# Expert layer of the second sequence and channel mix of the first, issued in pieces among the second attention's groups, with GELU and sigmoid written through tanh

## The chip, the cores and the metric

The kernel runs on one core of a Trainium2 chip. The metric is device time in microseconds (us): the median of the timed executions. A separate execution was recorded by the hardware profiler, and every duration and start time in this document comes from such a record.

The engines are named as in the profile: PE is TensorE (PEld its weight loads), DVE VectorE, ACT ScalarE, POOL GpSimd, and SP the engine that issues most of the DMAs. Each engine runs its own queue in order.

## The reference

Two sequences of 1024 tokens with 128 channels, all in f32, pass through four residual layers. Each layer reads a layer norm of x and adds its result to x.

```python
x = x + attn0(norm(x))   # 16 heads of 64, rotary embedding, full softmax over 1024 keys
x = x + ffn0(norm(x))    # 8 experts, each token goes to one:
                         #   y = gelu_tanh(t @ w1[e] + b1[e]) @ w2[e] + b2[e], times its route probability
x = x + attn1(norm(x))   # 16 heads of 8; keys of later 32-token windows get score 0 and still count
x = x + ffn1(norm(x))    # channel mix: r = sigmoid(xr @ W_r); k = relu(xk @ W_k)**2; r * (k @ W_v)
                         #   xr, xk blend each token with the one before it
```

GELU is the tanh approximation, 0.5 h (1 + tanh(sqrt(2/pi) (h + 0.044715 h^3))). The sigmoid equals 0.5 (1 + tanh(z/2)).

## The kernel before

The program is written with a tile framework. Python code issues instructions with tile names; a scheduler then fixes the order of each engine's queue from a cost model. Among the instructions that the model finds ready it takes the one issued first in the program. Tiles of one tag share a fixed number of buffers (`bufs`), and an instruction that needs a buffer still in use waits for the last reader. Semaphores are added by the framework.

**First attention** (`project`, `scores`, `flip`, `weighted`, `projected`). It walks 128 steps: 2 sequences x 8 head pairs x 8 query blocks. Beside the steps of the second sequence, the dictionary `beside` hangs the pieces of the expert layer of the first sequence, at hand-written step numbers.

**Expert layer** (`switch(b, ...)`). It returns three lists. `first_part` is `norm` (layer norm "f"), two `turn` pieces (transposes on PE), `route` (softmax over 8 experts and the argmax), `sort` (each token's slot in a list of 15 blocks of 128 rows), and eight `send` pieces: indirect DMAs from POOL that scatter 128 rows each into a DRAM tile `rows` (L298). `by_unit` has 8 units of two blocks (the last has one). In a unit `load` fetches the sorted rows (L310) and reads the block's expert number into a register of SP, with which it fetches 578 KB of weights per block (L314). `across` transposes the rows, `up` multiplies by w1 and adds the bias (L331), and after its last block runs GELU on ACT (L334). `down` multiplies by w2, adds the bias (L345) and stores to the DRAM tile `done` (L347). The third list gathers from `done` (`back`, L351) and adds to x (L356).

For the second sequence the same three lists run in a section of their own, between the two attentions, with two buffers of rows and four of weights.

**Second attention.** `prepare(b)` makes the layer norm "u", the q and k channels (`channels`, L649), splits each into three bf16 parts (`split`, L658 and L660), writes the parts to DRAM (`kept`, L666), and computes values and the sums for keys out of reach (`values`, `suffix`, `unreached`). `spread(n)` reads the parts back from DRAM in another layout, with 18 DMAs per group (L713). A group n is four heads of one sequence, so there are 8 groups. `maxima(n)` computes scores on PE and the row maxima on DVE (L738), and `rows_of` sends these by DMA into the `side` tiles (L758). `sums(n)` computes transposed scores `sT`, the exponentials on ACT (L782), and the weighted sums `o` on PE. `close(b)` divides and applies the output projection.

All of these pieces are placed by due times in a list `plan`, in units of a group: `maxima(n)` from n - 1.2 to n - 0.2, `sums(n)` from n to n + 1, and pieces of `prepare(1)` from 0.05 on. The list is sorted and issued. In this section every PE instruction is issued through `keep_in_program_order`, so the PE queue has exactly the order of the plan.

**Channel mix**, the last section: for each sequence a layer norm "z", transposes, two blends with the preceding token on DVE (L915, L917), three matrix products, relu and sigmoid on ACT (L924, L932), the square on POOL (L926), and the store.

Of the kernel before, what the change touches and what calls it, by code (L numbers as in the profile page):

```python
# [32 lines left out]
EPS = 1e-5  # L33
BIG = 1e30
# [3 lines left out]
def block_kernel(ctx: ExitStack, tc: tile.TileContext, t: dict, out: bass.AP):  # L38
# [27 lines left out]

    def mm(o, lhsT, rhs, start=True, stop=True):
        nc.tensor.matmul(o, lhsT, rhs, start=start, stop=stop)  # L68
# [92 lines left out]
    def transposed(xn, dst, name, affine=None):  # L161

        for g in range(2):
            pt = psum_t(f"pt_{name}_{g}")
            for c in range(4):
                nc.tensor.transpose(pt[:, c, :], xn[:, 4 * g + c, :], ident)
            o = dst[:, g * HALF : (g + 1) * HALF]
            i = pt.rearrange("p c k -> p (c k)")
            if affine is not None:
                nc.vector.tensor_scalar(o, i, affine[:, 0:1], affine[:, 1:2], ALU.mult, ALU.add)  # L170
            elif g == 0:
                nc.vector.tensor_copy(o, i)
            else:
                nc.scalar.copy(o, i)
# [16 lines left out]
    def switch(b, fp, deep):  # L191
# [6 lines left out]
        def r3(name, dtype=F32):  # L198
            return fp.tile([P, NCH, E], dtype, tag=name, name=f"{name}_{b}", bufs=1)
# [14 lines left out]
        def turn(g):  # L214
            pt = psum_t(f"pt_f_{b}_{g}")
            for c in range(4):
                nc.tensor.transpose(pt[:, c, :], state["xn"][:, 4 * g + c, :], ident)
            nc.scalar.copy(state["xT"][:, g * HALF : (g + 1) * HALF], pt.rearrange("p c k -> p (c k)"))

        def route():  # L220
# [20 lines left out]
            eq = r3("eq")  # L241
            tt(eq, prob, over_e(pmax), ALU.is_equal)
            cand = r3("cand")
# [7 lines left out]
        def sort():  # L251
# [16 lines left out]
            over = fp.tile([P, E, NCH], F32, tag="over", name=f"over_{b}", bufs=1)  # L268
# [3 lines left out]
            part = fp.tile([P, E, E], F32, tag="part", name=f"part_{b}", bufs=1)  # L272
# [5 lines left out]
            at = r3("at")  # L278
            nc.vector.scalar_tensor_tensor(at, over_c(begin), float(P), rank, ALU.mult, ALU.add)
            mine = r3("mine")  # L280
# [23 lines left out]
        ins, weights, xTs, hids = {}, {}, {}, {}  # L304

        def load(u):
            n = len(units[u])
            ins[u] = fp.tile([P, 2, D], F32, tag="rows", name=f"in_{b}_{u}", bufs=deep)
            k0 = units[u][0] * P
            nc.sync.dma_start(ins[u][:, :n], rows[k0 : k0 + n * P, :].rearrange("(c p) d -> p c d", p=P))  # L310
            for k in units[u]:
                e = nc.sync.value_load(state["whose"][0:1, k : k + 1], min_val=0, max_val=E - 1)
                weights[k] = fp.tile([P, FFN], F32, tag="wts", name=f"wts_{b}_{k}", bufs=2 + deep)
                nc.sync.dma_start(weights[k], t["ffn"][bass.ds(e, 1), :, :].rearrange("o p n -> (o p) n"))  # L314

        def across(u):
            n = len(units[u])
            pt = psum_t(f"pt_x_{b}_{u}")
            for i in range(n):
                nc.tensor.transpose(pt[:, i, :], ins[u][:, i, :], ident)  # L320
            xTs[u] = fp.tile([P, 2, P], F32, tag="xTs", name=f"xTs_{b}_{u}")
            nc.vector.tensor_copy(xTs[u][:, :n], pt[:, :n])
            hids[u] = fp.tile([P, 2, NFC, P], F32, tag="hid", name=f"hid_{b}_{u}", bufs=deep)

        def up(u, i):
# [7 lines left out]
            if i == n - 1:  # L333
                nc.scalar.activation(hids[u][:, :n], hids[u][:, :n], AF.Gelu_apprx_tanh)  # L334

        def down(u):
            n = len(units[u])
            py = psum_t(f"py_{b}_{u}")
            yo = fp.tile([P, 2, D], F32, tag="yrows", name=f"yo_{b}_{u}")
            for i, k in enumerate(units[u]):  # L340
# [4 lines left out]
                tt(yo[:, i, :], py[:, i, :], w[:, 2 * F + NFC :], ALU.add)  # L345
# [3 lines left out]
        def back(c):  # L349
            y = fp.tile([P, D], F32, tag="y", name=f"y_{b}_{c}", bufs=2 * deep)  # L350
            nc.gpsimd.indirect_dma_start(  # L351
                out=y, out_offset=None, in_=done[:, :],
                in_offset=bass.IndirectOffsetOnAxis(ap=state["place"][:, c : c + 1], axis=0),
            )
            xc = x[:, b * NCH + c, :]
            nc.vector.scalar_tensor_tensor(xc, y, state["gate"][:, c : c + 1], xc, ALU.mult, ALU.add)  # L356
# [6 lines left out]
            + [lambda u=u: down(u)]  # L363
            for u in range(len(units))
        ]
        return first_part, by_unit, [lambda c=c: back(c) for c in range(NCH)]
# [7 lines left out]
    with (  # L374
# [135 lines left out]
        early_part, units, back = switch(0, fp0, 1)  # L510
        at = NPAIR * NCH + NCH + LAG + 1
        for i, f in enumerate(early_part):
            beside.setdefault(at + (i if i < 5 else 5 + (i - 5) // 2), []).append(f)
        at += 13
        for u, fs in enumerate(units):
            for j, f in enumerate(fs):
                beside.setdefault(at + 5 * u + (-4 if j == 0 else 4 if j == len(fs) - 1 else j - 1), []).append(f)
# [23 lines left out]
        for work in later + sum(beside.values(), []) + back:  # L541
            work()

    first.close()

    with (
        tc.tile_pool(name="ffn", bufs=2) as fp0,
        tc.tile_pool(name="ps_t2", bufs=8, space=PSUM) as ps_t,
    ):
        banks.update(t=ps_t, w=ps_t)  # L550
        early_part, units, last = switch(1, fp0, 2)
        for f in early_part:
            f()
        for u in range(len(units) + 2):
            if u < len(units):
                units[u][0]()
            if 1 <= u <= len(units):
                for f in units[u - 1][1:-1]:
                    f()
            if u >= 2:  # L560
                units[u - 2][-1]()
        for f in last:
            f()
# [14 lines left out]
    with (  # L578
        tc.tile_pool(name="at1", bufs=2) as bp,
        tc.tile_pool(name="dr1", bufs=1, space=bass.MemoryType.DRAM) as dr1,  # L580
# [14 lines left out]
        def mm(o, lhsT, rhs, start=True, stop=True):  # L595
            return tc.keep_in_program_order(nc.tensor.matmul(o, lhsT, rhs, start=start, stop=stop))  # L596

        def flip1(o, i, one):
            return tc.keep_in_program_order(nc.tensor.transpose(o, i, one))
# [23 lines left out]
        def prepare(b):  # L623

            uT = acts.tile([P, N], F32, tag="xT", name=f"xT_u_{b}")
            work = []

            def norm():
                un = normed(b, "u")
                xs = x[:, seq(b), :]  # L630
                nc.gpsimd.tensor_tensor(xs, xs, bo1[:, None, :].to_broadcast([P, NCH, D]), ALU.add)
                for g in range(2):
                    work.insert(g, lambda g=g: turn(un, g))

            def turn(un, g):
                pt = psum_b(f"pt_u_{b}_{g}")
                for c in range(4):
                    flip1(pt[:, c, :], un[:, 4 * g + c, :], ident)
                nc.scalar.copy(uT[:, g * HALF : (g + 1) * HALF], pt.rearrange("p c k -> p (c k)"))

            full = {}

            def channels(which, g):
                if g == 0:
                    full[which] = bp.tile([P, N], F32, tag="full", name=f"full_{b}_{which}")
# [8 lines left out]
            def split(which):  # L654
                ps = [bp.tile([P, N], BF16, tag=f"part{which}{i}", name=f"part_{b}_{which}_{i}", bufs=1) for i in range(3)]
# [23 lines left out]
            def suffix():  # L679
                later = bp.tile([P, NCH - 1, H1, DA], F32, tag="later", name=f"later_{b}", bufs=1)  # L680
# [14 lines left out]
            work += [norm]  # L695
            work += [lambda w=w, g=g: channels(w, g) for w in range(2) for g in range(2)]
            work += [lambda w=w: split(w) for w in range(2)]
# [17 lines left out]
        def maxima(n):  # L715
# [35 lines left out]
            def rows_of():  # L751
# [3 lines left out]
                nT = bp.tile([3 * HG, N], BF16, tag="nT", name=f"nT_{n}")  # L755
# [14 lines left out]
        def sums(n):  # L770
# [29 lines left out]
            def turned(half):  # L800
# [9 lines left out]
                far = bp.tile([P, 4, HG, DA], F32, tag="far", name=f"far_{n}_{half}")  # L810
# [27 lines left out]
        def close(b):  # L838

            cx = cxs[b]  # L840
            cn = bp.tile([P, NCH, H1, DH1], F32, tag="cn", name=f"cn_{b}", bufs=1)

            def divide():
                r = small.tile([P, NCH, H1], F32, tag="r1", name=f"r1_{b}")
# [8 lines left out]
            def turn1(g):  # L853
                pc = psum_b(f"pc_{b}_{g}")
                for c in range(4):
                    flip1(pc[:, c, :], cn[:, 4 * g + c].rearrange("p h d -> p (h d)"), ident)
                cTs[g] = bp.tile([P, 4, P], F32, tag="cT", name=f"cT_{b}_{g}")
# [10 lines left out]

        def run(work):
# [4 lines left out]

        AHEAD = 0.2
        work = prepare(0)
        run(work)
        for n in range(2):
            spread(n)
        plan = []  # L880
        for n in range(B * NG):
            plan += [(n - 1 - AHEAD + at, f) for at, f in maxima(n)]
            plan += [(n + at, f) for at, f in sums(n)]
            if n >= 2:
                plan.append((n - 2 + 0.3, lambda n=n: spread(n)))
        work = prepare(1)

        def first_of_second():
            work.pop(0)()

        plan += [(0.05 + 0.055 * i, first_of_second) for i in range(len(work) + 2)]
        plan += [(NG + 0.4 + 0.05 * i, f) for i, f in enumerate(close(0))]
        plan.sort(key=lambda e: e[0])
# [3 lines left out]


    with (
        tc.tile_pool(name="ffn1", bufs=2) as gp,  # L900
        tc.tile_pool(name="ps_s3", bufs=2, space=PSUM) as ps_s,
        tc.tile_pool(name="ps_t3", bufs=2, space=PSUM) as ps_t,
        tc.tile_pool(name="ps_m3", bufs=2, space=PSUM) as ps_m,
    ):
        banks.update(s=ps_s, t=ps_t, m=ps_m)
        rest = gp.tile([P, 2], F32, tag="rest", name="rest", bufs=1)
        nc.vector.tensor_scalar(rest, mu, -1.0, 1.0, ALU.mult, ALU.add)
        for b in range(B):
            zT = gp.tile([P, N + 1], F32, tag="zT", name=f"zT_{b}")
            nc.gpsimd.memset(zT[:, 0:1], 0.0)  # L910
            transposed(normed(b, "z"), zT[:, 1:], f"z_{b}")
            mix = []
            for w in range(2):
                prev = gp.tile([P, N], F32, tag=f"prev{w}", name=f"prev{w}_{b}")
                nc.vector.tensor_scalar_mul(prev, zT[:, :N], rest[:, w : w + 1])  # L915
# [118 lines left out]
```

## Time and profile before

| what | us |
|---|---|
| median of 3 runs (1522.61 to 1526.13) | 1526.01 |
| profiled execution, its own time | 1524.13 |
| its span, first to last instruction | 1522.3 |
| end of the last score matrix work of attention 1 (last `ptt`) | about 1007 |
| first `in<-rows` load of the second sequence's experts | 1061.7 |
| last `py` matmuls of that expert layer | 1138.8 |
| first `sT` matmul of the second attention | 1206.9 |
| last `oS` copy of the second attention | 1482.2 |

Busy shares over the span: PE 89%, DVE 61%, ACT 48%, POOL 28%. To read the profile: a row of instructions gives line, engine, operation, the tile written and the tiles read, the count, busy time and mean duration, and then how long the engine stood idle before them and what ended that idle time. PEclk is the clock that PE was granted, as a fraction of full speed; matmul durations at a clock below 1 are longer. PE's busy time is modelled, so 90% does not mean that PE works at its peak.

### The profile page before, as it was taken

How to read it: one execution, taken by the hardware profiler on the slowest of the kernel's cores; microseconds unless marked ns; L12 is line 12 of the kernel's file. 1: busy time of each engine (PE TensorE's matmuls, PEld its weight loads, DVE VectorE, ACT ScalarE, POOL GpSimd, SP SyncE). 2: the span in 40 equal slices, each digit the busy share in tenths (PEclk: the TensorE clock that was granted, in tenths of full speed). 3: DMA queues.
4: the chain of work that ended last, by engine and by line, in shares of the span. 5: the costliest groups of instructions: out<-in, count | busy, mean ns of one | idle time of the engine just before them, and what ended most of it. 6: DMA issues, size and time to landing. Idle time of an engine off the chain costs nothing.

```text
span 1522.3 us, 22391 instructions
## 1 busy us (share of the span) xinstructions
PE 1350.8 (89%) x8418; PEld 773.9 (51%) x8418; DVE 923.2 (61%) x1859; ACT 737.1 (48%) x1383; POOL 429.9 (28%) x422
## 2 busy tenths in 40 slices
PE   3999999999999999999999999980674889898975
PEld 2455565565565565565666666660562233333324
DVE  6656665666666666656555565652225886787716
ACT  0555455455545555455554555640112166666672
POOL 2443434333443333453332332232005010000001
PEclk9999999999999999999999999985676599999997
DMA  5000000000000000100111111002334222211000
GB/s 182 1 2 0 1 1 1 1 1 1 1 1 1 1 1 1 55 11 5 39 39 39 39 39 37 5 17 83 110 107 141 45 65 38 44 33 33 2 2 28
DMA packets 34037, 47.61 MB, mean 31 GB/s; under 512 B 4101, under 2 KB 22021, under 8 KB 33801
## 3 DMA queue, kind: packets, MB, share of 16 engines
q1 hardware_dynamic: 32329, 42.50, 10.0%
q0 software_dynamic: 1024, 2.10, 0.4%
q8 instruction: 67, 1.10, 0.3%
q10 hardware_dynamic: 576, 1.57, 0.3%
q14 instruction: 41, 0.34, 0.1%
HBM read 36.79 MB, written 9.18 MB: 30 GB/s over the span
## 4 chain that ended last, share of the span: by engine, by line
PE 77%; DMA 7%; DVE 7%; ACT 5%; issue 2%; POOL 1%; SPq 0%; POOLq 0%; ACTq 0%; DVEq 0%
PE ptt L467 16%; PE s L68 16%; PE ov L68 15%; PE pq L68 8%; PE o L596 4%; ACT pT L782 3%; PE s L596 3%; PE sT L596 3%; DVE nm L738 2%; PE py L68 2%; PE pv L68 2%; PE ph L68 2%; DMA wts<-in_ffn 2%; PE y L68 2%; DMA rows<-xn_f,place 1%
## 5 line engine op out<-in xcount | busy, mean ns | idle before, releaser
L443 DVE TENSOR_SCALAR_CACHE_REDUCE neg<-s 128x1024 f32<-128x1024 f32 x256 | 303.3, 1222 | 222.6 <-PE s L68 222.6
L447 ACT ACTIVATE p<-neg,nm 128x1024 f32<-128x1024 f32 x256 | 293.2, 1147 | 234.5 <-DVE neg L443 232.7
L452 POOL TENSOR_SCALAR p<-p,r 128x1024 f32<-128x1024 f32 x256 | 283.9, 1122 | 353.5 <-PE ptt L467 227.6
L467 PE MATMUL ptt<-ident,p 128*128 128x128 f32 x2048 | 269.2, 280 | 3.2 <-POOL p L452 2.0
L68 PE MATMUL s<-qkT,qkT 64*128 64x512 f32 x1024 | 259.9, 615 | 0.7 <-DVE neg L443 0.6
L467 PEld LDWEIGHTS ptt<-ident,p 128*128 128x128 f32 x2048 | 219.1, 140 | 75.6 <-issue 49.2
L68 PE MATMUL ov<-pT,v 128*64 128x256 f32 x2048 | 255.7, 386 | 0.0
L470 DVE COPY pT<-ptt 128x512 f32<-128x512 f32 x256 | 177.1, 692 | 120.0 <-PE ptt L467 112.4
L738 DVE TENSOR_REDUCE nm<-s 128x1 f32<-128x640 f32 (+7 forms) x176 | 175.3, 1025 | 59.2 <-PE s L596 57.6
L472 ACT COPY pT<-ptt 128x512 f32<-128x512 f32 x256 | 148.3, 586 | 114.8 <-PE ptt L467 114.2
L782 ACT ACTIVATE pT<-sT 128x512 f32<-128x512 f32 (+3 forms) x384 | 161.8, 493 | 84.5 <-PE sT L596 83.5
L68 PEld LDWEIGHTS ov<-pT,v 128*64 128x64 f32 x2048 | 138.5, 136 | 97.2 <-issue 31.1
L417 POOL TENSOR_TENSOR qkT<-rp,rp 128x512 f32<-128x512 f32 x64 | 81.6, 1275 | 255.5 <-DVE rp L412 251.0
L68 PEld LDWEIGHTS s<-qkT,qkT 64*128 64x128 f32 x1024 | 89.5, 186 | 84.0 <-issue 81.8
L596 PEld LDWEIGHTS <-side 107*128 107x128 bf16 (+1 forms) x768 | 66.4, 100 | 129.0 <-issue 86.8
L596 PE MATMUL sT<-side,side 107*128 107x512 bf16 (+3 forms) x384 | 99.7, 330 | 19.5 <-ACT pT L782 16.2
L596 PE MATMUL s<-side,side 104*128 104x512 bf16 (+3 forms) x384 | 99.4, 359 | 11.4 <-DMA side<-kept 5.9
L412 DVE SCALAR_TENSOR_TENSOR rp<-pq,rope 128x512 f32<-128x512 f32 x128 | 85.2, 685 | 2.3 <-PE pq L68 2.1
L811 POOL TENSOR_TENSOR far<-oor,en 128x144 f32<-128x144 f32 x16 | 7.0, 441 | 273.1 <-ACT en L809 208.6
L596 PE MATMUL o<-pT,v 128*32 128x512 f32 (+3 forms) x768 | 81.8, 499 | 0.0
L68 PE MATMUL pq<-xT_a,w_qkv 128*128 128x512 f32 x128 | 72.4, 648 | 0.0
L68 PE MATMUL pq<-xT_a,w_swap 128*128 128x512 f32 x128 | 68.9, 620 | 0.0
(173 smaller groups left out, 1015.6 us busy)
## 6 DMA issues: line engine op xcount, KB each, us to landing
wts<-in_ffn SPq DMA_DIRECT2D x30, 578.0 KB
side<-kept SPq DMA_DIRECT2D x144, 64.0 KB
kept<-part SPq DMA_DIRECT2D x12, 256.0 KB
rows<-zero SPq DMA_DIRECT2D x2, 960.0 KB
in<-rows SPq DMA_DIRECT2D x14, 128.0 KB
done<-yo SPq DMA_DIRECT2D x14, 128.0 KB
w_qkv<-in_w_qkv ACTq DMA_DIRECT2D x3, 512.0 KB
x<-in_x SPq DMA_DIRECT2D x2, 512.0 KB
```

Source lines behind the costliest of these rows:

```text
L68: nc.tensor.matmul(o, lhsT, rhs, start=start, stop=stop)
L412: nc.vector.scalar_tensor_tensor(part, pq, DH0 ** -0.5 if which == 0 else 1.0, rope[:, s, tok], ALU.mult, ALU.mult)
L417: nc.gpsimd.tensor_tensor((qT, kT)[which][:, tok], parts[0], parts[1], ALU.add)
L443: nc.vector.tensor_scalar(neg, s[:, j].rearrange("p g k -> p (g k)"), -1.0, None, ALU.mult, ALU.min, accum_out=nm)
L447: nc.scalar.activation(p, neg, AF.Exp, bias=nm, scale=-1.0, accum_out=sums[:, j : j + 1])
L452: nc.gpsimd.tensor_scalar(out[j], out[j], r[:, j : j + 1], 1.0, ALU.mult, ALU.mult)
L467: nc.tensor.transpose(pt[:, c, :], probs[j][:, c0 : c0 + P], ident)
L470: nc.vector.tensor_copy(o, pt)
L472: nc.scalar.copy(o, pt)
L596: return tc.keep_in_program_order(nc.tensor.matmul(o, lhsT, rhs, start=start, stop=stop))
L738: nc.vector.tensor_reduce(o, sv, AX.X, ALU.max, negate=True)
L782: nc.scalar.activation(pT[:, :w], s[:, :w], AF.Exp)
```

## The change

1. The section between the attentions is gone. The first sequence's `back` and its layer norm "u" (now a function `enter`) are put among the last steps of the first attention, and the expert units there are 4 steps apart instead of 5.
2. The second sequence's `first_part` is issued in turn with the second half of `prepare(0)`. Its 8 units get due times from -0.78 to 1.82 in the plan, its gathers and additions follow, then `enter(1)` and `prepare(1)` from 2.17 to 3.2.
3. GELU by one ACT instruction becomes a chain of five: Square on ACT, two POOL instructions, Tanh on ACT, one on DVE. The sigmoid of the channel mix becomes Tanh with scale 0.5, its factor and sum folded into DVE instructions that were there.
4. The store of a unit's result is a piece of its own, a fifth of a unit after `down` (one step later in the first attention). The gathers are split from the additions.
5. `mix(b)` is the channel mix in 11 pieces; those of sequence 0 are due from 4.8 on, 0.12 apart, and those of sequence 1 run at the end. The first factor of a blend moves from DVE to POOL.
6. Expert matmuls, transposes and channel mix in this section also go through `keep_in_program_order` and take their PSUM tiles from the three `ps1_t` banks that `sT` uses. Several tiles share tags or lose their second buffer to fit (`full`, `part`, `hid`, `xTs`, `rows`, `nT`, `far`).

```diff
 ...
+    def pe(i):
+        return tc.keep_in_program_order(i) if in_order[0] else i
+
     def mm(o, lhsT, rhs, start=True, stop=True):
-        nc.tensor.matmul(o, lhsT, rhs, start=start, stop=stop)
+        pe(nc.tensor.matmul(o, lhsT, rhs, start=start, stop=stop))
 ...
-            ins[u] = fp.tile([P, 2, D], F32, tag="rows", name=f"in_{b}_{u}", bufs=deep)
+            ins[u] = fp.tile([P, 2, D], F32, tag="rows", name=f"in_{b}_{u}", bufs=1)
 ...
-                weights[k] = fp.tile([P, FFN], F32, tag="wts", name=f"wts_{b}_{k}", bufs=2 + deep)
+                weights[k] = fp.tile([P, FFN], F32, tag="wts", name=f"wts_{b}_{k}", bufs=3 + b)
 ...
-            if i == n - 1:
-                nc.scalar.activation(hids[u][:, :n], hids[u][:, :n], AF.Gelu_apprx_tanh)
+            if i < n - 1:
+                return
+
+            h = hids[u][:, :n].rearrange("p i c k -> p (i c k)")
+            g = fp.tile([P, 2 * NFC * P], F32, tag="gel", name=f"gel_{b}_{u}", bufs=1)[:, : n * NFC * P]
+            nc.scalar.activation(g, h, AF.Square)
+            nc.gpsimd.tensor_scalar(g, g, GELU_A, 1.0, ALU.mult, ALU.add)
+            nc.gpsimd.tensor_tensor(g, g, h, ALU.mult)
+            nc.scalar.activation(g, g, AF.Tanh, scale=GELU_C)
+            nc.vector.scalar_tensor_tensor(h, g, 1.0, h, ALU.add, ALU.mult)
 ...
-                tt(yo[:, i, :], py[:, i, :], w[:, 2 * F + NFC :], ALU.add)
+                nc.vector.scalar_tensor_tensor(
+                    yo[:, i, :], py[:, i, :], 0.5, w[:, 2 * F + NFC :], ALU.mult, ALU.add
+                )
+            outs[u] = yo
+
+        def store(u):
 ...
+            for f, j in zip(fs, (-4, 0, 1, 2, 4, 5) if len(fs) == 6 else (-4, 0, 1, 4, 5)):
+                put(at + 4 * u + j, f)
+        at += 4 * len(units) + 2
+        for c, f in enumerate(back):
+            put(at + c // 4, f)
 ...
+        put(at + 4, enter_first)
 ...
-    with (
-        tc.tile_pool(name="ffn", bufs=2) as fp0,
-        tc.tile_pool(name="ps_t2", bufs=8, space=PSUM) as ps_t,
-    ):
 ...
+        def mix(b):
 ...
+            def blend(w):
+                m = whole(f"mix{w}")[:, :N]
+                nc.gpsimd.tensor_scalar(m, big["zT"][:, :N], rest[:, w : w + 1], 1.0, ALU.mult, ALU.mult)
+                nc.vector.scalar_tensor_tensor(m, big["zT"][:, 1 : N + 1], mu[:, w : w + 1], m, ALU.mult, ALU.add)
 ...
+                nc.scalar.activation(big[hf][:, 1], pr.rearrange("p c k -> p (c k)"), AF.Tanh, scale=0.5)
 ...
-        work = prepare(0)
-        run(work)
+        early_part, units, back = switch(1, fp1)
+        work = prepare(0, uTs[0])
+        run(work[:6])
         for n in range(2):
             spread(n)
+        rest_of = work[6:]
+        for i in range(max(len(rest_of), len(early_part))):
+            for w in (early_part, rest_of):
+                if i < len(w):
+                    w[i]()
 ...
-                plan.append((n - 2 + 0.3, lambda n=n: spread(n)))
 ...
+                plan.append((n - 2 + (0.5 if n == NG else 0.3), lambda n=n: spread(n)))
+        at, long = -0.5, 0.28
+        for u, fs in enumerate(units):
+            for f, j in zip(fs, (-1, 0.0, 0.25, 0.5, 1.1, 1.3) if len(fs) == 6 else (-1, 0.0, 0.25, 1.1, 1.3)):
+                plan.append((at + (u + j) * long, f))
+        at += (len(units) + 0.4) * long
+        plan += [(at + (0.03 * c if c < NCH else 0.16 + 0.01 * c), f) for c, f in enumerate(back)]
+        at += 0.16 + 0.02 * NCH
 ...
+        plan.append((at, enter_second))
+        plan += [(at + 0.01 + 0.03 * i, lambda: second["in"].pop(0)()) for i in range(3)]
+        at += 0.11
+        plan += [(at + 0.04 * i, lambda: second["rest"].pop(0)()) for i in range(6 + 2 * NCH + 1)]
         plan += [(NG + 0.4 + 0.05 * i, f) for i, f in enumerate(close(0))]
+        plan += [(NG + 0.8 + 0.12 * i, f) for i, f in enumerate(mix(0))]
 ...
         run(close(1))
 ...
+        run(mix(1))
```

## The prediction

> **What bounds the kernel now.** I read the windows view first (busy time of each engine by stretch), then the timeline of the stretch between the attentions, then the chain that ended last and the groups of one steady group of the second attention. Columns of the windows: start and end, length, then PE, PEld, DVE, ACT, POOL busy with counts, granted PE clock, DMA share, GB/s.
>
> ```profile
> 900.00:1000.00 100.00, 100.00 (x677) 63.16 (x674) 61.44 (x118) 59.04 (x97) 31.37 (x28) 1.00 0.06 18
> 1000.00:1060.00 60.00, 21.30 (x159) 17.70 (x157) 22.51 (x98) 10.22 (x18) 19.56 (x19) 0.67 0.18 58
> ...
> 1100.00:1120.00 20.00, 11.53 (x59) 10.73 (x60) 3.70 (x7) 1.80 (x2) 0.00 (x0) 0.71 0.43 136
> ...
> 1160.00:1180.00 20.00, 9.00 (x44) 7.23 (x44) 8.64 (x18) 4.53 (x10) 6.74 (x10) 0.67 0.60 189
> ...
> 1272.00:1304.50 32.50, 29.24 (x212) 10.93 (x208) 24.37 (x39) 21.09 (x53) 0.87 (x2) 1.00 0.21 38
> ```
>
> The first attention fills PE wholly at full clock. From about 1007 to 1207 us, between the attentions, PE is half idle and its clock falls to 0.67. One group of the second attention (last row) takes 32.5 us, with PE busy for 29.2, DVE 24.4 and ACT 21.1. So 200 us are serial, and in the rest PE leads with the others not far behind.
>
> The chain (start, us, what) shows what the serial stretch waits for:
>
> ```profile
> 1059.48 2.22 DMA rows<-xn_f,place
> ...
> 1088.90 5.33 DMA wts<-in_ffn
> ...
> 1144.14 0.95 POOL y L351
> ...
> 1155.87 10.92 DMA kept<-part
> ...
> 1167.54 3.64 DMA side<-kept
> ...
> 1208.30 0.59 PE sT L596
> ```
>
> It is DMA latency: eight scatters (1037.1 to 1061.7), weights for each unit (5.3 us of waiting per unit), gathers (1141.6 to 1151.3), the bounce of q and k through DRAM (1155.9 to 1178.1), and then a maxima pass alone (1178.1 to 1206.9), which DVE bounds with 21.5 us of reductions.
>
> **Part 1: the stretch before the first sT.** Before, it ends at 1206.9. After, only `prepare(0)`, its spreads and the first maxima have to come first. Attention 1 ends with its last projection at 1015.4; I add 2 us for `enter(0)` and `back(0)` in it (eight transposes 1.1 us, and table loads). The transposes and the layer norm have other PE work beside them there. `channels` and `split` then take as long as from 1153.3 to 1178.1, 25 us to the first score. But PE's order now puts the sort's matmuls, the values and `unreached` ahead of the first score. From the first st_f (1013.6) to `place` (1036.2) the routing took 22.6 us; then come four values (about 2 us), `suffix` on POOL (0.3 + 4.1 us), between scatters that hold POOL's queue for 2.5 to 5 us each, and `unreached` (about 5 us). I take the first score at 1052 rather than at 1043. Maxima 24 us, one unit's DVE work 3.6 us (0.42 + 2 x 0.69 + 1.28 + 2 x 0.29), a wait of 5 for that unit's GELU chain, and 8 for `rows_of`, its DMA (1204.2 to 1208.3 before) and leftovers: first sT at 1093. Gain 1206.9 - 1093 = **114 us**; bounds 127 (nothing held by the sort) and 95 (POOL's scatters hold `suffix` and the scattered rows arrive late at `across`).
>
> The sends, loads and stores move too. SP's queue gets `in<-rows` and two weight DMAs ahead of `side<-nT`; the sends end near 1039 + 25 = 1064, about when `across(0)` comes up, so I count no more for it.
>
> **Part 2: PE work that enters the groups.** One block is 8 `ph` records in 1.13 us and 8 `py` in 1.16, both at full clock, a unit's transposes 0.38. Units 1 to 7 lie behind the first sT: 13 blocks x 2.29 + 7 x 0.38 = 32.4. Channel mix of one sequence: pk 1.02, w_r 1.05, w_v 1.16 for each half, transposes 1.1: 7.6. Sum **+40 us**, since PE is the engine with least idle time. The other engines keep room: per unit DVE gets 3.6, ACT 2 x 1.06, POOL 3.5 us.
>
> **Part 3: waits that PE's fixed order adds.** In a unit `down` comes 0.6 x 0.28 = 0.168 group after the last `up`: 5.5 us of a 32.5 us group, and the next unit's transposes 0.4: 5.9. The chain from `up` to `down` is hid add 0.69, Square 1.06 (the Gelu row's time), POOL tensor_scalar 1.12 (row p<-p,r), POOL tensor_tensor 2.35 (row x<-x,bo), Tanh 1.06, DVE 1.28 (row mix), half a us of handovers, and about 1.6 in the queues of DVE (75% busy) and ACT (65%): 9.6. PE waits 3.7 us per unit, and behind it stand the next sT and scores. Units 1 to 6: **+22**; bounds 0 (if the work of neighbours is ahead) and 45. These rows are the instructions of the chain, or ones of the same shape:
>
> ```profile
> L452 POOL TENSOR_SCALAR p<-p,r 128x1024 f32<-128x1024 f32 x256 | 283.9, 1122 | 353.5 <-PE ptt L467 227.6
> ...
> L631 POOL TENSOR_TENSOR x<-x,bo 128x1024 f32<-128x1024 f32 x2 | 4.7, 2346 | 12.0 <-DVE xn_u L149 12.0
> ...
> L917 DVE SCALAR_TENSOR_TENSOR mix<-zT,mu,prev 128x1024 f32<-128x1024 f32 x4 | 5.0, 1279 | 0.0
> ```
>
> From the last `down` (1.77) to the transposes of norm "u" (2.21) the plan has 0.44 group, 14 us. The chain there is store 2.5, eight gathers 10, landing 2.3, addition and statistics 1, square root with its table load 2, first normed blocks 1.5, queues 3: about 22 to 24 us. **+10**, and 2.6 for two table loads that delay the exponentials. Layer norm "z" of sequence 0 has 9.6 us of plan between `out1` and its transposes for a chain of about 12: +3. The second spread has 0.32 group after the last split (10 us and 5 of added work) for some 20 us of bounce: +3, since values and `unreached` stand between. Against this, a PE wait lets ACT and DVE catch up, of whose lateness PE loses 3.2 us per group now: -8. Sum of part 3: **+33**. Three shared PSUM banks may cost more (31 expert tiles, each 0 to 0.7 us), or nothing; I take 0 and keep 20 for the high end.
>
> **Part 4: table loads and stores.** Gelu and Exp alternate now: 9 loads for L334, 10 for L447, 1.28 us each. With tanh these are to vanish. In the first attention PE is at 100 of 100 us, so ACT's relief is worth 0; the POOL work there (3.5 us per unit beside 31 of 100 busy) delays a `p` by at most 2.4 us, and `ptt` waited for POOL only 2.0 us in all: 0 to +6, within the 2 us of part 1. The delayed stores keep SP from standing in front of `yo`: 0, as SP's waits now are in front of idle time.
>
> [...]
>
> **Part 5: the tail.** From the last `oS` copy to the end the kernel takes 1522.3 - 1482.2 = 40.1 us now, with both sequences' mixes mingled. Alone, sequence 1 needs 9.6 for close, about 8 for norm "z", 1.5 for transposes and copies, 2.4 for the blend, 8 to the last addition with its second half behind, 3.5 for the store: 32. Gain **8** (4 to 12).
>
> **Sum** against the profiled execution: 1524.1 - 114 + 40 + 33 - 8 = 1475. The median of the runs lies 1.9 above that execution, and I add 3 for half of the bank term's middle: **1480 us**.
>
> **The rivals.**
> - *The waits do not appear, the gain is larger.* If the neighbours' work covers GELU and gather chains as it does in the first attention (PE 100 of 100 us with the same pieces beside), part 3 goes to 0 or below and the first score comes at 1043: 1524 - 123 + 40 - 8 = 1433. For: DVE and ACT have room. Against: there the plan leaves two steps, 15 us, for the chain, here 5.9. Chance 0.27.
> - *The start is not overlapped.* Sort, scatters and `suffix` on one POOL queue hold the first scores until the scatters end (1064) and `unreached` after: first sT near 1115, 1502 us. Chance 0.18.
> - *Slower: the weight DMAs come late in PE's fixed order.* A pair is issued when `down` of two units before frees its buffers, 0.32 group ahead of its use: 10.5 us, and 5 to 9 of added work. The pair needs 6.7 us now (issued 1075.86, second block's matmuls at 1082.61), with little else moving; 18 `side<-kept` DMAs move as many bytes (1.15 MB) on the same queue, which makes 13. If SP stands blocked besides, each of 7 units waits. From 6.6 us per unit (46 / 7) the kernel is no faster; at 12 us it takes 1480 + 84 = 1564. For: units waited 5.3 us each before. Against: the lead is twice as long now. Chance 0.10.
> - My forecast, 1455 to 1500: 0.45.
>
> Faster by over 0.3% (4.6 us, about what a measurement of this kernel can tell): all but the slower rival and a little of the second, 0.87; within 0.3%: 0.03; slower: 0.10. The range runs from the first rival's value to just below the old time, 1430 to 1520.
>
> **What would show it.** Right: first sT near 1093; no Gelu loads; PE idle ahead of `py` ended by DVE `hid`, 3 to 4 us per unit; idle ahead of `pt_u` of sequence 1 near 10; PE clock 1.0 throughout the units; tail near 32. Wrong: idle ended by DMA `wts` or `in` of over 6 us per unit; first sT after 1110; first-attention end after 1022; groups 0 to 2 longer than 60 us or under 45.

## The result and the profile after

The changed kernel takes **1572.6 us** (median of 4 runs, 1570.87 to 1578.41) against 1526.07 for the kernel before (4 runs): 1.0317 of its time, 95% interval 1.0286 to 1.0347. 1480 was predicted, with 1430 to 1520 as the range. The profiled execution took 1570.87 us (span 1568.9).

The span falls into four stages: attention 1 up to its last projection (`y<-w_out,oT`), from there to the first `sT`, the groups of the second attention to the last `oS` copy, and the tail. Each border is the start of the instruction named. The last column belongs to the best kernel of the experiments below (e15).

| stage, us | before | after | predicted change | measured change | e15 |
|---|---|---|---|---|---|
| attention 1 | 1015.1 | 1072.5 | +2 | **+57.4** | 1021.7 |
| to the first `sT` | 191.8 | 91.9 | -116 | -99.9 | 91.9 |
| groups | 275.3 | 370.6 | +73 | **+95.3** | 343.3 |
| tail | 40.1 | 33.9 | -8 | -6.2 | 34.4 |
| span | 1522.3 | 1568.9 | -49 | +46.6 | 1491.3 |

The serial stretch did become shorter by 100 us, but the two stages that took the work in became longer by 153. Windows view of the changed kernel (columns as in the prediction):

```profile
700.00:800.00 100.00, 93.53 (x533) 55.34 (x532) 53.33 (x97) 42.94 (x72) 35.19 (x30) 0.91 0.10 30
...
1072.80:1164.40 91.60, 47.64 (x217) 32.25 (x218) 50.61 (x102) 12.18 (x22) 23.71 (x29) 0.65 0.45 112
1164.40:1535.00 370.60, 299.50 (x1923) 136.27 (x1922) 217.44 (x395) 201.72 (x455) 47.24 (x51) 0.90 0.20 46
600.00:1072.80 472.80, 442.97 (x2695) 268.17 (x2691) 268.10 (x541) 215.65 (x372) 183.36 (x156) 0.95 0.09 26
```

The two last stretches in the kernel before (here the groups come first):

```profile
1206.90:1482.20 275.30, 243.81 (x1676) 94.42 (x1676) 184.21 (x318) 181.21 (x432) 9.35 (x21) 0.99 0.16 33
600.00:1015.40 415.40, 413.23 (x2685) 257.87 (x2681) 251.70 (x501) 222.90 (x375) 153.56 (x137) 1.00 0.09 29
```

In attention 1 PE issues about as many matmuls as before (2695 for 2685 records), but is busy for 443 us instead of 413, stands idle for 30 instead of 2, and its mean clock is 0.95. So the loss has two halves: waits, and matmuls that take longer at a lower clock. The timeline of one expert unit beside attention 1 (start, duration, engine, instruction; in brackets the idle time before it and what ended it) shows both:

```profile
715.11 1.05 ACT L347 ACTIVATE gel<-hid 128x1024 f32<-128x1024 f32 x1
...
717.22 1.99 PE L74 MATMUL s<-qkT,qkT 64*128 64x512 f32 x8
...
718.12 1.05 POOL L348 TENSOR_SCALAR gel<-gel 128x1024 f32<-128x1024 f32 x1
...
719.25 2.36 POOL L349 TENSOR_TENSOR gel<-gel,hid 128x1024 f32<-128x1024 f32 x1
...
721.64 1.06 ACT L350 ACTIVATE gel<-gel 128x1024 f32<-128x1024 f32 x1 [3.73 <-POOL gel L349]
722.07 0.86 PEld L514 LDWEIGHTS ptt<-ident,p 128*128 128x128 f32 x8 [0.39 <-issue]
722.07 1.09 PE L514 MATMUL ptt<-ident,p 128*128 128x128 f32 x8
722.73 1.23 DVE L351 SCALAR_TENSOR_TENSOR hid<-gel,hid 128x1024 f32<-128x1024 f32 x1 [5.28 <-ACT gel L350]
723.88 1.22 DVE L490 TENSOR_SCALAR_CACHE_REDUCE neg<-s 128x1024 f32<-128x1024 f32 x1
...
726.39 2.03 PE L74 MATMUL s<-qkT,qkT 64*128 64x512 f32 x2 [3.23 <-DVE neg L490]
...
728.36 1.97 PE L514 MATMUL ptt<-ident,p 128*128 128x128 f32 x8
...
730.25 3.44 PE L74 MATMUL s<-qkT,qkT 64*128 64x512 f32 x6
```

The scores `s` of the step are ready at 719.2, and DVE has been idle since 717.5. But the last instruction of the GELU chain, `hid` (L351), stands ahead of `neg` in DVE's queue. It waits 5.28 us for the chain of Square, two POOL instructions and Tanh, and `neg`, on which the softmax of the step hangs, runs 4.7 us late. PE finds nothing to do for 3.23 us. In the kernel before, where GELU needs no DVE step, this `neg` starts as soon as its scores are there:

```profile
718.15 1.23 DVE L443 TENSOR_SCALAR_CACHE_REDUCE neg<-s 128x1024 f32<-128x1024 f32 x1 [1.80 <-PE s L68]
```

Then comes the second half: eight `ptt` records take 1.97 us, where eight took 1.09 at 722.07. The granted clock is 0.50 from about 726.4 to 733.2, and normal durations return at 733.6. The windows view of this place, of an idle time with the clock still at 1.00 (it ended at 809.65), and of a stretch behind the idle time that ended at 1032.26:

```profile
726.40:733.20 6.80, 6.80 (x16) 3.19 (x16) 1.90 (x4) 2.43 (x5) 2.22 (x2) 0.50 0.00 0
...
807.00:810.00 3.00, 0.35 (x1) 0.29 (x2) 3.00 (x6) 1.61 (x3) 0.00 (x0) 1.00 0.00 0
...
1033.70:1037.00 3.30, 3.30 (x9) 1.21 (x7) 1.64 (x7) 2.28 (x4) 2.22 (x2) 0.50 0.02 5
```

### The profile page after: what moved, and what is told of

It reads as the page before. It is cut to its first block, busy times and chain, and to the rows that moved or that the text cites. A ratio compares the mean times of both kernels' runs of the same rounds, so it can differ in the third digit from the quotient of the medians.

```text
span 1568.9 us, 22384 instructions
## 1 busy us (share of the span) xinstructions
PE 1381.1 (88%) x8418; PEld 782.3 (50%) x8418; DVE 934.7 (60%) x1869; ACT 737.0 (47%) x1386; POOL 487.4 (31%) x458
## 4 chain that ended last, share of the span: by engine, by line
PE 69%; DVE 8%; issue 6%; POOL 6%; ACT 5%; DMA 5%; SPq 0%; POOLq 0%; ACTq 0%; DVEq 0%
PE s L74 18%; PE ptt L514 15%; PE ov L74 13%; PE pq L74 7%; PE o L74 4%; PE sT L74 3%; DMA rows<-xn_f,place 3%; PE pv L74 3%; ACT pT L809 2%; DVE neg L490 2%; POOL gel L349 2%; PE y L74 2%; PE py L74 1%; POOL p L499 1%; DVE nm L765 1%
## 5 line engine op out<-in xcount | busy, mean ns | idle before, releaser
L74 PE MATMUL s<-qkT,qkT 64*128 64x512 f32 x1024 | 282.0, 637 | 16.4 <-DVE neg L490 16.4
L514 PE MATMUL ptt<-ident,p 128*128 128x128 f32 x2048 | 276.3, 283 | 15.2 <-DVE rp L459 10.3
L514 PEld LDWEIGHTS ptt<-ident,p 128*128 128x128 f32 x2048 | 223.4, 142 | 97.2 <-issue 55.8
L74 PEld LDWEIGHTS s<-qkT,qkT 64*128 64x128 f32 x1024 | 95.8, 192 | 106.5 <-issue 104.3
L74 PE MATMUL sT<-side,side 107*128 107x512 bf16 (+3 forms) x384 | 106.5, 342 | 31.6 <-ACT pT L809 24.5
L74 PE MATMUL o<-pT,v 128*32 128x512 f32 (+3 forms) x768 | 87.0, 528 | 0.0
L74 PE MATMUL py<-wts,hid 128*128 128x128 f32 x240 | 43.8, 339 | 16.6 <-DVE hid L351 13.9
```

The source lines that it names most:

```text
L74: pe(nc.tensor.matmul(o, lhsT, rhs, start=start, stop=stop))
L514: nc.tensor.transpose(pt[:, c, :], probs[j][:, c0 : c0 + P], ident)
```

## The experiments

Theory A: the place of the chain's last step in DVE's queue costs the time in attention 1. Theory B: the 3.5 us that each unit adds on POOL do, through the `p` of the softmax. Theory C: the units come too densely there, 4 steps apart instead of 5. All experiments are edits of the changed kernel; ratios are to the kernel before, with 95% intervals.

**e2: GELU as one ACT instruction again**, in both layers.

```diff
-            if i < n - 1:
-                return
 ...
-            nc.scalar.activation(g, h, AF.Square)
 ...
+            if i == n - 1:
+                nc.scalar.activation(hids[u][:, :n], hids[u][:, :n], AF.Gelu_apprx_tanh)
```

> The changed kernel with GELU as the one ACT instruction again, in both expert layers (table loads return). Theory A (the last DVE step of the tanh chain stands in DVE's queue ahead of the next step's neg, so PE waits for the whole chain): the first attention, whose last y ended at 1072 us, ends near 1034 (eight units at about 5 us each, PE's clock dips included); the kernel takes about 1530. Theory B (POOL's extra 3.5 us per unit delays the probabilities): the same here. Theory C (units 4 steps apart instead of 5 crowd PE): the end stays near 1070 and the kernel near 1570.

Measured 1510.59 us, 0.9894 (0.9868 to 0.9921): 62 us below the changed kernel, and faster than the one before. Attention 1 ends at 1026.5 instead of 1072.5, and the groups take 360.8 instead of 370.6. So GELU by tanh, as the changed kernel issues it, is what made the change slower. C falls, since the units are still 4 steps apart. A and B both stand, because this edit removes the DVE step and the POOL work together.

**e3: gathers, joins and layer norm "u" after the loop.**

```diff
-        for c, f in enumerate(back):
-            put(at + c // 4, f)
 ...
-        for work in later:
+        uTs[0], ins0 = enter(0)
+        for work in later + back + ins0:
```

> The changed kernel with the first sequence's gathers, additions and layer norm u issued after the first attention's loop instead of in its last eight steps. Theory A (the additions and the norm stand ahead of neg on DVE, the gathers ahead of p on POOL): the loop gets about 15 us shorter, the gathers and the norm cost about 9 after it, net 1564 to 1568. Rival: gathers in the loop were nearly free and become serial: 1580 or more.

Measured 1579.32 us, 1.0332 (1.0294 to 1.037). The 1564 to 1568 of theory A did not come. The experiment did not move what it was to move: the scheduler put the gathers on POOL at 1019.2 to 1028.1 all the same, since they were ready, and PE's waits in attention 1 stayed (15.7 us on `neg` against 15.8). The layer norm alone became later, by 4 us.

**e4: Tanh and the DVE product as a piece of their own**, issued one step later; **e6: e4 and e3 together.**

```diff
+            gels[u] = g, h
+
+        def finish(u):
+            g, h = gels.pop(u)
             nc.scalar.activation(g, g, AF.Tanh, scale=GELU_C)
             nc.vector.scalar_tensor_tensor(h, g, 1.0, h, ALU.add, ALU.mult)
 ...
-(-4, 0, 1, 2, 4, 5)
+(-4, 0, 1, 2, 3, 4, 5)
```

> The changed kernel with the same five GELU instructions, but the last two (Tanh on ACT, the product on DVE) as a piece of its own, issued one step later in the first attention and 0.35 of a unit later in the second. Theory A (queue position): the first attention ends near 1038, the kernel takes about 1535. Theory B (POOL's time itself, unchanged here) and theory C (spacing): 1570 to 1575.

> Both: the last two GELU instructions as a later piece, and the first sequence's gathers, additions and norm after the loop. Theory A: the two add up, about 1528. Theory B: 1565 to 1570.

Measured 1573.8 (1.0318, 1.029 to 1.0346) and 1574.68 (1.0322, 1.0296 to 1.0349). That looks like B, but DVE's part of the timeline in e4 says otherwise:

```profile
722.83 1.23 DVE L355 SCALAR_TENSOR_TENSOR hid<-gel,hid 128x1024 f32<-128x1024 f32 x1 [5.26 <-ACT gel L354]
723.97 1.22 DVE L494 TENSOR_SCALAR_CACHE_REDUCE neg<-s 128x1024 f32<-128x1024 f32 x1
```

The product stands directly ahead of `neg` again, and in e6 as well (722.14). The edit changed the program and not the queue, so neither run tells A from B.

**e7: as e4, with both instructions pinned**, so that they can't go ahead of what the program issued before them.

```diff
-            nc.scalar.activation(g, g, AF.Tanh, scale=GELU_C)
-            nc.vector.scalar_tensor_tensor(h, g, 1.0, h, ALU.add, ALU.mult)
+            tc.keep_in_program_order(nc.scalar.activation(g, g, AF.Tanh, scale=GELU_C))
+            tc.keep_in_program_order(nc.vector.scalar_tensor_tensor(h, g, 1.0, h, ALU.add, ALU.mult))
```

> As e4_gelu_split, but the late piece's Tanh and product are also pinned behind what the program issues before them on ACT and DVE (e4's DVE queue came out in the order of the changed kernel, so its piece had not moved at all). The same instructions, POOL's share included; in the first attention the product now stands behind the next step's two neg instead of ahead of them. Theory A (queue position): the first attention ends near 1030 us instead of 1072, the kernel takes about 1530. Theory B (POOL's time): 1570.

Measured 1527.42 us, 1.0005 (0.9989 to 1.0021). Attention 1 ends at 1026.1. The same five instructions run, the POOL work included; only the place of the last two differs. This shows A. (The pin moved Tanh in ACT's queue as well. In the changed kernel, the next work there, the exponential `p`, started at 725.13 when `neg` was there, 2.4 us after Tanh had ended, so Tanh held nothing back.) From e7's DVE timeline and its windows:

```profile
719.28 1.23 DVE L494 TENSOR_SCALAR_CACHE_REDUCE neg<-s 128x1024 f32<-128x1024 f32 x1 [1.80 <-PE s L74]
...
724.27 1.65 DVE L355 SCALAR_TENSOR_TENSOR hid<-gel,hid 128x1024 f32<-128x1024 f32 x1
```

```profile
700.00:800.00 100.00, 100.00 (x641) 62.10 (x639) 65.12 (x119) 50.82 (x86) 48.53 (x38) 1.00 0.13 38
600.00:1026.40 426.40, 418.50 (x2699) 258.79 (x2695) 271.19 (x542) 214.68 (x372) 190.27 (x156) 0.99 0.10 29
```

`neg` runs as soon as its scores are there, the product 5 us later, and PE is at 100 of 100 again, with POOL busier (48.5 of 100) than in the changed kernel. Against that kernel, attention 1 has 21.9 us less idle time and 24.5 us less busy time on PE, together the 46.4 by which it is shorter. Clock times busy time, taken in slices of 0.5 us, puts 18.6 of the 24.5 down to the lower clock; the other 6 stay open (the busy time is modelled).

**e8: e7, and the gathers two per step instead of four, the joins pinned, the norm two steps later.**

```diff
-            put(at + c // 4, f)
+            put(at + (c // 2 if c < NCH else 2 + (c - NCH) // 2), f)
 ...
-        put(at + 4, enter_first)
+        put(at + 6, enter_first)
```

> e7 with the first sequence's gathers two per step instead of four, their additions pinned two steps later, and the transposes of norm u after the loop. If the gathers and additions cost the other 10 us or so of the first attention: 8 to 10 below e7. If not: within 3 of e7.

Measured 1518.04 us, 0.9943 (0.9924 to 0.9961): 9.4 below e7, the number expected, though only a part of it came from where it was expected. The stretch in question, as the timeline of the changed kernel has it:

```profile
1024.54 0.95 POOL L376 DMA_INDIRECT y<-done,place  x1 [0.30 <-issue]
1024.62 0.35 DVE L383 SCALAR_TENSOR_TENSOR x<-y,pmax,x 128x128 f32<-128x128 f32 x1 [0.92 <-DMA y<-done,place]
...
1025.52 2.22 POOL L499 TENSOR_SCALAR p<-p,r 128x1024 f32<-128x1024 f32 x2
1025.82 2.33 DVE L383 SCALAR_TENSOR_TENSOR x<-y,pmax,x 128x128 f32<-128x128 f32 x2 [0.84 <-DMA y<-done,place]
...
1029.76 1.20 DVE L490 TENSOR_SCALAR_CACHE_REDUCE neg<-s 128x1024 f32<-128x1024 f32 x1
...
1032.26 1.09 PE L74 MATMUL s<-qkT,qkT 64*128 64x512 f32 x2 [3.81 <-DVE neg L490]
```

Eight gathers in a row on POOL hold back a `p`, and the joins and statistics on DVE hold back a `neg`. In e8 PE has no wait on `neg` left there (its waits on `p` went from 3.7 to 5.2), and attention 1 ends 2.7 us earlier (1023.4). That is no more than four kernels with the same pieces in attention 1 differ by (e10, e12, e13, e15: 1019.0 to 1021.8). Another 8 us came in the groups, where PE is busy for 4 us less and idle for 4 us less: a wait of 5.5 on `nm` is gone and `side<-kept` makes it wait 9.7 instead of 11.0, while `pt_u` waits 1.9 longer. What links this to the gathers stayed open.

**e9: start reordered** (`suffix` issued ahead of the scatters), units from -0.2 on, 0.24 apart; **e10: e2, e8's gathers and e9 together.**

```diff
+        for w in rest_of[5:] + early_part[5:]:
+            w()
 ...
-        at, long = -0.5, 0.28
+        at, long = -0.2, 0.24
```

> The changed kernel with the suffix sums and unreached issued ahead of the eight scatters, and the expert units 0.3 group later and 0.24 instead of 0.28 apart. If the scatters on POOL's queue held the first score (PE stood 21.7 us at the suffix sums): first score about 40 us after the first attention's end instead of 48, first sT about 80 after it instead of 92, the kernel near 1560. If the side DMAs or the maxima set it anyway: 1572 to 1576.

> The single GELU instruction of e2 with the gathers of e8 and the order of e9. If all three add up: 1511 - 9 - 12 = 1490. If only the gathers help: 1502.

Measured 1567.07 (1.0262, 1.0242 to 1.0282) and 1506.38 (0.9871, 0.9851 to 0.989). In both, `suffix` ran behind four scatters as before, so the reordering was not tried by them, and e10 missed both of its numbers. The first `sT` came 10.9 us earlier (81.0) because the units came later, and the groups took 10.6 longer (e9): a shift. e9's median is 5.5 us below the changed kernel's all the same. Its profiled execution is only 1.8 shorter, 1.5 of it in attention 1, so the profile does not show where the rest comes from.

**e11: the scatters pinned behind `suffix`.** In the changed kernel PE waits 21.7 us for `later`, which `suffix` writes on POOL after the fourth scatter (timeline of PE):

```profile
1115.47 0.85 PE L74 MATMUL pl<-later,ones 128*128 128x144 f32 x2 [21.71 <-POOL later L711]
...
1138.14 0.66 PE L77 MATMUL pt_x<-ident,in 128*128 128x128 f32 x2 [2.12 <-DMA in<-rows]
```

```diff
+            if b:
+                tc.keep_in_program_order(i)      # i: the indirect DMA of send
 ...
+        for w in rest_of[5:9] + early_part[5:] + rest_of[9:]:
+            w()
```

> The changed kernel with one thing else: the eight scatters of the second sequence are pinned on POOL behind `suffix` (issued in the order: first five early pieces in turn with five values, the other three values, `suffix`, the scatters, `unreached`). Theory S, that the first score waits because `suffix` stands behind four scatters on POOL: the PE wait of 21.7 us on `later` goes, `pl` is done some 30 us after the end of attention 1, and the next thing that is late is group 0's `side<-kept` (landed about 39 us after that end in the changed kernel); first maxima at 39 to 41 instead of 48.6, and the whole 8 us shorter, about 1564. Rival: the DMA queue, with 35 `side<-kept` and the scatters on it, is the bound anyway; the first maxima move by under 3 us, 1570 to 1573.

Measured 1579.3 us, 1.0358 (1.0328 to 1.0388): slower, outside both expectations. The same lines in e11:

```profile
1101.17 0.85 PE L74 MATMUL pl<-later,ones 128*128 128x144 f32 x2 [7.84 <-POOL later L713]
...
1116.31 2.16 PE L74 MATMUL s<-side,side 104*128 104x128 bf16 x10 [9.63 <-DMA side<-kept]
...
1144.48 0.66 PE L77 MATMUL pt_x<-ident,in 128*128 128x128 f32 x2 [12.08 <-DMA in<-rows]
```

The wait on `later` went down as it should, and two others took its place: first the bounce, then the scattered rows, which now arrive later, because the first scatter starts at 1101.8 instead of 1094.7. The wait of 21.7 us that looked like the cause lay beside the real path, the scatters. (In the changed kernel the chain that ended last goes through all eight of them, 0.3 us apart, to the first weights.)

**e12: e2, e8's gathers and e11 together; e13: e12 with the units 0.24 apart.**

```diff
-        at, long = -0.5, 0.28
+        at, long = -0.5, 0.24
```

> The three repairs together: GELU as the one ACT instruction, two gathers per step with pinned joins, scatters pinned behind `suffix`; units as in the changed kernel. If the three add up (1510.6 for GELU alone, 9.4 for the gathers, 8 for the scatters) 1493; if the scatters bring nothing (rival) 1501. Below 1506.4 either way.

> As the one before, with units 0.24 group apart instead of 0.28 (first due time unchanged), so that everything behind the last unit, with the second sequence's spread, comes 0.32 group or 10 us earlier. If the wait of 11 us for `side<-kept` of the second sequence is what counts, it goes below 3 and the time falls by 8, to 1485. Rival: the units stand too close, every chain from `up` to `down` has 0.8 us less and each unit waits more, as in the run with 0.24 before (groups 10 us longer): 1500.

Measured 1505.67 (0.9857, 0.983 to 0.9884) and 1497.92 (0.9809, 0.9785 to 0.9833). e12 is above both of its numbers, about as e11's cost would have it: 1510.6 - 9.4 + 6.7 = 1508. e13 is its expected 8 us below e12, and the wait that was to go is gone. Waits of PE in the groups (who waits, for whom, us in total, times, longest), in e12:

```profile
PE s L74 <- DMA side<-kept: 10.1, 1, 10.1
```

and the largest ones in e13, where this wait does not occur any more:

```profile
PE sT L74 <- ACT pT L801: 29.7, 52, 4.4
PE pt L77 <- ACT oS L816: 8.2, 12, 1.2
PE pt_u L77 <- DVE xn_u L158: 6.0, 1, 6.0
```

**e14 and e15: the second group's 18 `side<-kept` issued behind the load of the first rows**, in the changed kernel and in e13.

```diff
-        for n in range(2):
-            spread(n)
+        spread(0)
 ...
+        plan.append((-0.73, lambda: spread(1)))     # its DMAs pinned on SP
```

> The changed kernel with `spread(1)` (18 of the 35 `side<-kept` of the start) issued behind `load(0)` on SP, pinned there; nothing else. If the transfers beside them are what makes a scatter take 7.5 us instead of 2.5, the last four scatters go at 2.5 each and the last one lands near 52 us after the end of attention 1 instead of 63. `suffix` still stands behind four scatters, so the first score stays where it is; the two PE waits of 2.1 (`in<-rows`) and 1.9 (`wts`) go: first `sT` 4 us earlier, about 1569. Rival (the scatters are slow for another reason): 1573, scatters end where they did, and if spread(1) is then late for group 1's maxima 1576.

> The run with units 0.24 apart, GELU as one instruction, spread gathers and `suffix` first (1497.9), and `spread(1)` held back as well. If scatters slowed by transfers set the start: the scatters end some 10 us earlier, the wait on `in<-rows` goes, the first `sT` comes 84 to 87 us after the end of attention 1 instead of 96, and the time is 1486 to 1489. Rival (something else holds the start, or the groups give it back): 1495 to 1499.

Measured 1569.92 (1.0291, 1.0263 to 1.032) and **1491.44** (0.977, 0.9745 to 0.9795), the fastest of all. The chains, of the changed kernel and then of e15 (start, duration up to the landing):

```profile
1098.06 4.74 DMA rows<-xn_f,place
1103.06 7.48 DMA rows<-xn_f,place
1110.81 7.49 DMA rows<-xn_f,place
1118.56 7.49 DMA rows<-xn_f,place
1126.32 4.33 DMA rows<-xn_f,place
1130.92 2.23 DMA rows<-xn_f,place
```

```profile
1052.68 7.89 DMA rows<-xn_f,place
1060.84 5.48 DMA rows<-xn_f,place
1066.58 2.22 DMA rows<-xn_f,place
1069.07 2.21 DMA rows<-xn_f,place
```

The scatters are slow while `side<-kept` are on their way: these are issued from 1098.3 to 1124.2 in the changed kernel, from 1048.7 to 1059.5 in e15, and after that a scatter takes 2.2 us again. e14, which moves 18 of these 35 transfers and nothing else, shows it: the other 17 are issued from 1098.1 to 1109.0, the last four scatters follow each other every 2.5 us, and the last is issued at 1123.7 instead of 1133.4. That moved the first `sT` of e14 by only 1.4 us, since there `suffix` still holds the first scores; its median is 2.7 below the changed kernel's, which the intervals don't separate. In e15, where `suffix` is first, the first `sT` comes 4.3 us earlier than in e13 and the whole is 6.5 faster, short of the expected 9 to 12: the second unit's rows, now behind the 18 transfers on SP, cost a wait of 4.7 us.

## Why the prediction was wrong, point by point

**Part 4, the step that failed.** It took the GELU chain beside attention 1 as POOL work that delays a `p` by at most 2.4 us ("0 to +6, within the 2 us of part 1"). The cost was 46.4 us (e7 against the changed kernel), and not by POOL. The step left out that the chain ends on DVE, in a queue that also holds `neg`. Part 3 reckoned exactly this kind of chain, 9.6 us, for the groups. For attention 1 I relied on the 15 us that the plan leaves before `down`; but the plan orders only the program, and the scheduler put the product into DVE's queue ahead of the next step's two `neg` instead of behind them (e4 and e7 show the two orders). The first rival rested on the same argument (PE at 100 of 100 with the same pieces beside), which was true of a GELU in one ACT instruction. The prediction's own sign of being wrong, an end of attention 1 after 1022, came up.

**The clock.** Nothing in the sum allowed for it. In attention 1, seven waits of 2.8 to 3.2 us (21.5 in sum: 12.0 on `neg` outside the gather stretch, 9.5 on `rp`) went with 24.5 us of longer busy time, of which the clock explains 18.6. Here these waits cost about twice their length.

**Part 1, `enter(0)` and `back(0)` "2 us".** With GELU's share taken off, attention 1 still ends 11 us later than before (1026.1). e8's spreading gave 2.7 of it back, e10's and e12's 7.5 and 4.7 (1019.0 and 1021.8 against 1026.5 in e2), where the pieces in attention 1 are the same in both. In e12 PE still waits 5.2 us for `p` and 1.5 for `pT` there (1.6 and 0.3 in the kernel before). The rest is not settled.

**Part 1, first `sT` 76 us after attention 1.** It came after 91.9. I had the scatters at 25 us, as in the kernel before; they took 41, from 1094.7 to 1135.7. The second rival had the right place (sort, scatters, `suffix`), but with the scatters at their old duration.

**Parts 2 and 3, the groups, +73 by 40 of work and 33 of waits.** Busy time times clock, in slices of 0.5 us, is 240 us before and 271 after. That splits the 56 us of longer busy time into some 31 of added work instead of 40 (`ph` of two of the 13 blocks, 2.3 us, came before the first `sT`) and some 25 of lower clock that had no term; "PE clock 1.0 throughout the units" was wrong (0.90 over the groups). The waits rose by 39.6 (idle 31.5 to 71.1), near the 33, but by other parts:

```profile
PE sT L74 <- ACT pT L809: 24.5, 48, 4.4
PE s L74 <- DMA side<-kept: 11.0, 1, 11.0
...
PE py L74 <- DVE hid L351: 8.4, 4, 3.5
...
PE pt_u L77 <- DVE xn_u L158: 2.0, 1, 2.0
```

The GELU chain made PE wait 8.4 us in the groups (22 predicted), the gather chain 2.0 (10 predicted), the second sequence's bounce 11.0 (3 predicted). The exponentials, for which I had subtracted 8, went up from 16.2 to 24.5. In e2, with the table loads back (by the count: its ACT runs 1402 instructions, 16 more than in the changed kernel, with 16 fewer for GELU), they are at 38.4 and no `py` waits for `hid`, yet the groups are 9.8 us shorter: that is what the tanh form cost there in all.

**Right:** the tail (33.9, 32 predicted), no Gelu table loads (the kernel before has 29 table loads of 1.28 us, 9 of them for Gelu; the changed kernel has 14, none of them at the GELU lines L347 and L350), weights hardly waited for (1.9 us at the first unit), so the slower rival's mechanism did not occur; the kernel was slower by another one. And e15, with GELU in one instruction and the start and the gathers put right, takes 1491.44: moving the work is worth 35 us, where 46 were predicted.

**Sums and readings that were off, with little effect.** The terms of part 5 add up to 33.0, not 32 (measured 33.9). Half of the bank term's middle, 31 tiles x 0.35 / 2, is 5.4, not 3. The 5.3 us read as each unit's wait for weights are the length of a transfer in the chain; PE's waits on `wts` in the kernel before are 22.0 us in sum, over six units.

## What to carry to other kernels

Before an edit replaces one instruction by a chain across engines, ask in which queue its last step stands and what critical instruction is behind it there; duration and load of the engines say nothing on that. If a scheduler fixes the queues, moving a piece in the program may leave its instructions where they were (e3, e4, e9): read the new trace's order, and pin the instruction. A long wait that one line reports (21.7 us on `later`) may be only the last of several that end close together; before counting on it, look for what arrives next.

## What the runs showed of the hardware

- After an idle time of 3.23 us, which ended at 726.39 in the changed kernel, PE's granted clock was 0.50 for 6.8 us. After one of 3.81, which ended at 1032.26, it stayed at 1.00 until about 1033.6 and was 0.50 from there to 1037.1, for 3.4 us. After one of 2.76, which ended at 809.65, it stayed at 1.00; after another of 2.76, which ended at 968.95, it was 0.50 for 6.8 us (from 968.75 on). So the length of an idle time alone did not decide it here.
- One scatter of 128 rows took 7.5 to 8.0 us while the 64 KB `side<-kept` transfers were on their way (changed kernel: 7.48 from 1103.06; e15: 7.89 from 1052.68; in e11 the first four started 8.2 to 8.3 apart, from 1101.81), and 2.2 behind them (changed kernel: 2.23 from 1130.92; e15: 2.22 from 1066.58).
- Two joins on DVE (0.35 us each elsewhere) took 2.33 together in the changed kernel, from 1025.82 to 1028.15, beginning 0.3 us after a POOL `p` of 2.22 and ending 0.4 after it. The timeline does not show what made them longer.
